# A margin on the operand's due time for steps queued beside a selective scan (one Trainium2 core)

## The chip, the core and the metric

The kernel runs on one core of a Trainium2 chip. The metric is the device time of one execution in microseconds: 9593.26 us is the median of three runs of the kernel before (9591.71 to 9620.02). The profiled execution spans 9618.0 us.

A core has engines with one instruction queue each: PE (matrix multiply), DVE (vector), ACT (scalar functions), POOL (GpSimd) and SP (here it only issues transfers). The order of the instructions in each queue is fixed when the program is built.

## What is computed

The input x has 4 images of 96 channels and 64 x 64 pixels. Four layers follow one another, each added to its input:

```python
x = x + L0(group_norm(x))     # in-projection, 3x3 depthwise conv, selective scan, gate, out-projection
x = x + L1(group_norm(x))     # deformable 3x3 convolution: offsets and mask, bilinear gather, conv
t = t + Fourier(layer_norm(t)); t = t + ffn(layer_norm(t))            # layer 2, on tokens
t = t + linear_attention(layer_norm(t)); t = t + ffn(layer_norm(t))   # layer 3
```

The core of L0 is a recurrence along 4096 positions, for 4 directions k, 192 channels d and 16 states n:

```python
dA = exp(delta * A);  h = dA * h + (delta * u) * B;  y = sum_n(h * C)
```

## The kernel before

**The scan.** `Layer0.scan` (line 776) cuts the recurrence into units of 8 channels x 16 states (128 partitions) by 1024 positions. For each image b, in the order of the directions k = 1, 3, 0, 2, there are 4 steps of 1024 positions by 24 units: 4 x 4 x 4 x 24 = 1536 units. A unit is one instruction or two on each engine: ACT makes the decay `da` by an exponential (866), PE spreads the inflow `db` (872), DVE multiplies it by B (885) and runs the scan (888), POOL saves the last state (895) and multiplies by C (897), and PE adds up over the states (915). Decay and inflow are queued a unit ahead, the product with C two units behind.

**The two streams.** All other work is in two streams of generators made in `layers23`. `ends()` (1617) makes the inputs of the scan for images 0, 1, 2, 3 (`Layer0.before`) and then takes layers 2 and 3 of images 0 to 3 (`Layers23.image`). `middle()` (1627) clears the tables and then for each image takes what follows the scan (`Layer0.behind`) and layer 1 (`Layer1.image`, whose gathers are issued by POOL). A stream gives steps: a few instructions with a cost in us for each engine, `cost(pe, dve, act, pool)`. Most loops are a `pipe` (261) of several chains of such steps, which picks the first chain whose next step may go. A chain may also wait for tokens of buffers (`takes`, `frees`); `Layer0.before` has chains of eight working steps over five chains in flight, with three buffers `ex`, one `lw`, two `rl` and two `du`.

**The clock.** `Clock` (203) holds for each engine the time `ends[engine]` at which what is queued on it will be done, by the written costs. The engines are numbered PE, DVE, ACT, POOL = 0 to 3. After each unit `unit()` moves the due time by PACE = 4.9 and sets `idle`, the end of the scan queued last or the due time, if that is later. Then both streams queue steps until neither has one that may go (`while go()`), and the next unit is queued. When a step may go is told by `has_room` (226): DVE work beside a unit is at most BESIDE = 6.0; the operand (`ready`, the time at which the step before it in its chain is done) must be there when its first engine comes to it, which is the later of `ends[first]` and `idle`; and each engine that it uses may be at most AHEAD (2.0, 1.5, 3.0, 4.0) beyond `now()`. The first engine is looked for in the order PE, ACT, DVE, POOL: a step with PE work has PE as its first engine, a step with ACT and DVE work has ACT.

**Alone.** Before the scan's inputs are there, and after its last unit, `alone()` queues steps by a clock of its own (`clock.own` is a number and not None). After the last unit the streams also get five more PSUM banks. The lists of instructions end up in each queue in the order in which they were made (`in_program_order`).

Lines that the steps below name: 744, 745 and 747 (`w`, `lw`, `rl`), 762 to 768 (`du` in three bf16 parts) in `Layer0.steps`; 1218 and 1227 (gather and its weights) and 1241 and 1249 (transposes and their copy) in `Layer1.sample`; 1417 and 1419 (the last product of the Fourier layer and its addition to t); 1538 (keys and values of the attention, 32 copies for each image).

Of the kernel before, what the change touches and what calls it, by code (L numbers as in the profile page):

```python
# [194 lines left out]

AHEAD = (2.0, 1.5, 3.0, 4.0)

BESIDE = 6.0

PACE = 4.9  # L200
# [2 lines left out]
class Clock:  # L203
# [22 lines left out]
    def has_room(self, work, ready):  # L226
        now = self.now()
        idle = self.idle if self.own is None else self.own
        if self.own is None and work[DVE] and self.beside >= BESIDE:
            return False  # L230
        first = next((e for e in (PE, ACT, DVE, POOL) if work[e]), None)
        if ready > (now if first is None else max(self.ends[first], idle)):
            return False
        return all(not w or e <= now + a for w, e, a in zip(work, self.ends, AHEAD))

# [1450 lines left out]
```

## Time and profile before

| what | value |
|---|---|
| time, median of three runs | 9593.26 us |
| span of the profiled execution | 9618.0 us, 92316 instructions |
| mean granted PE clock | 0.767 |
| scan instructions (line 888) | 1152 of 2347 ns and 384 of 2287 ns, from 356.4 to 8187.7 us |
| product with B (line 885) | 1536 of 1215 ns |
| product with C (line 897) | 1536 of 2389 ns |
| gathers (line 1218) | 1152 of 1228 ns, from 2731.5 to 8839.9 us |

A page of the profile gives the busy time of each engine and then the span in 40 slices, with a digit for the busy tenths of each slice; a slice here is 240 us. The views of the waits say for an engine and line what ended its idle time: "DVE du L768 <- ACT du L766" is DVE standing idle with line 768 at its head until ACT finished line 766. The view of windows gives busy us and instruction counts of each engine in a stretch of time, then the granted PE clock, the share of the transfer engines and GB/s.

### The profile page before, as it was taken

The page shows a single profiled execution, that of the slowest core. Times are in us where ns is not written, and L with a number is a line of the kernel's source. Part 1 is how long each engine was busy: PE and PEld are TensorE (multiplying, and loading weights), DVE is VectorE, ACT ScalarE, POOL GpSimd, SP SyncE. Part 2 cuts the span into 40 slices and gives each one's busy share as a digit, 9 for nine tenths or more (in the row PEclk, how much of TensorE's full clock was granted, in tenths as well). Part 3 has the DMA queues.
Part 4 walks back from the last instruction along what each step waited for, and adds up shares of the span by engine and source line. Part 5 has one row for each costly group of instructions (what it writes and reads, how often), then busy time and mean ns, then how long its engine had stood idle before and what let it go on. Part 6 is the DMA issues. An engine that isn't in the chain of part 4 may idle for free.

```text
span 9618.0 us, 92316 instructions
## 1 busy us (share of the span) xinstructions
PE 6838.2 (71%) x31928; PEld 3124.9 (32%) x31928; DVE 7027.1 (73%) x4707; ACT 4082.4 (42%) x5574; POOL 6730.8 (70%) x4947
## 2 busy tenths in 40 slices
PE   6465855696756667867565787777767787788787
PEld 2111311131212233312122454323335542377474
DVE  0488778877888888778888887788878888332313
ACT  3563656465544333555433233453332345311323
POOL 0696589766889999678899995566989656376101
PEclk8555966696767678967666787877878887989887
DMA  1466676776777778777777787767777776354010
GB/s 48 139 188 168 172 189 193 184 185 177 207 195 191 204 200 206 189 183 205 195 199 203 195 212 172 182 159 190 192 189 198 192 184 168 86 145 130 16 54 11
DMA packets 775819, 1609.47 MB, mean 167 GB/s; under 512 B 247666, under 2 KB 338830, under 8 KB 773239
## 3 DMA queue, kind: packets, MB, share of 16 engines
q10 hardware_dynamic: 300672, 985.79, 40.5%
q1 hardware_dynamic: 400950, 391.20, 14.9%
q0 software_dynamic: 73728, 226.57, 8.8%
q8 instruction: 254, 4.16, 0.2%
q14 instruction: 215, 1.75, 0.1%
HBM read 1346.94 MB, written 256.29 MB: 167 GB/s over the span
## 4 chain that ended last, share of the span: by engine, by line
POOL 29%; PE 25%; DVE 16%; DMA 14%; issue 8%; ACT 5%; ACTq 1%; SPq 1%; DVEq 0%; POOLq 0%
POOL hh L897 13%; POOL g L1218 7%; DVE hh L888 7%; DMA da<-de 4%; DVE db L885 4%; PE pc L657 4%; PE ps L1241 3%; PE f L1332 3%; PE py L915 2%; PE db L872 2%; POOL lw L745 2%; DMA du<-du 2%; PE po L1118 2%; POOL st L895 1%; POOL w L744 1%
## 5 line engine op out<-in xcount | busy, mean ns | idle before, releaser
L897 POOL TENSOR_TENSOR hh<-hh,bc 128x1024 f32<-128x1024 f32 x1536 | 3667.4, 2389 | 341.8 <-DVE hh L888 229.2
L888 DVE TENSOR_TENSOR_SCAN hh<-da,st,db 128x1024 f32<-128x1024 f32 x1152 | 2703.7, 2347 | 365.0 <-ACT da L866 196.7
L872 PE MATMUL db<-du,rep 96*128 96x512 bf16 x3072 | 1172.9, 473 | 1531.8 <-DVE hh L888 1372.3
L866 ACT ACTIVATE da<-da,w_al 128x1024 f32<-128x1024 f32 x1536 | 1734.3, 1145 | 816.8 <-DMA da<-de 457.0
L885 DVE TENSOR_TENSOR db<-db,bc 128x1024 f32<-128x1024 f32 x1536 | 1866.9, 1215 | 278.0 <-PE db L872 275.9
L1218 POOL DMA_INDIRECT g<-table,idx x1152 | 1414.1, 1228 | 308.6 <-issue 226.8
L915 PE MATMUL py<-hh,w_fold 128*32 128x512 f32 x6144 | 1226.2, 809 | 121.6 <-POOL hh L897 98.8
L872 PEld LDWEIGHTS <-rep 96*128 96x128 bf16 x3072 | 275.4, 106 | 2633.9 <-issue 1521.2
L1241 PE MATMUL ps<-w_ident,g 128*96 128x128 f32 x4608 | 729.7, 325 | 342.8 <-DVE g L1227 180.7
L888 DVE TENSOR_TENSOR_SCAN hh<-da,db 128x1024 f32<-128x1024 f32 x384 | 878.1, 2287 | 125.4 <-ACT da L866 73.8
L1227 DVE TENSOR_TENSOR g<-g,wt 128x3456 f32<-128x3456 f32 x128 | 550.6, 4302 | 377.8 <-DMA g<-table,idx 361.4
L1241 PEld LDWEIGHTS ps<-w_ident,g 128*96 128x96 f32 x4608 | 639.6, 153 | 533.6 <-DVE g L1227 231.3
L895 POOL COPY st<-hh 128x1 f32<-128x1 f32 x1152 | 314.6, 273 | 642.6 <-DVE hh L888 619.1
L1249 ACT COPY st<-ps 96x384 f32<-96x384 f32 x384 | 182.1, 476 | 1182.8 <-PE ps L1241 1108.8
L657 PE MATMUL pc<-pad,wc 96*128 96x512 f32 x1152 | 544.0, 620 | 49.2 <-DMA wc<-wc_d 43.7
L1478 POOL CAST xqf<-fl 96x512 fp8e5<-96x512 f32 x64 | 51.2, 806 | 733.3 <-DVE fl L1436 635.5
L744 POOL TENSOR_TENSOR w<-w,ex 128x512 f32<-128x512 f32 x192 | 248.2, 1293 | 383.7 <-ACT w L741 383.2
L915 PEld LDWEIGHTS py<-hh,w_fold 128*32 128x32 f32 x6144 | 173.8, 126 | 719.6 <-issue 372.9
L768 DVE TENSOR_TENSOR du<-ex,du 128x512 bf16<-128x512 f32 x192 | 266.1, 1386 | 190.2 <-ACT du L766 186.6
L734 PE MATMUL pd<-xd,w_dtw 103*64 103x512 f32 (+1 forms) x512 | 316.3, 922 | 68.1 <-DMA w_dtw<-in_dtw 32.0
L747 DVE SCALAR_TENSOR_TENSOR rl<-pd,lw 128x512 f32<-128x512 f32 x192 | 130.0, 677 | 301.3 <-POOL lw L745 296.2
L657 PEld LDWEIGHTS pc<-pad,wc 96*128 96x128 f32 x1152 | 222.8, 198 | 344.6 <-issue 327.4
(241 smaller groups left out, 9366.1 us busy)
## 6 DMA issues: line engine op xcount, KB each, us to landing
da<-de ACTq DMA_DIRECT2D x1536, 512.0 KB
du<-du ACTq DMA_DIRECT2D x384, 192.0 KB
bc<-bcd ACTq DMA_DIRECT2D x128, 512.0 KB
du<-du SPq DMA_DIRECT2D x128, 384.0 KB
y<-yb SPq DMA_DIRECT2D x384, 128.0 KB
de<-rl SPq DMA_DIRECT2D x128, 256.0 KB
m<-in_dft SPq DMA_DIRECT2D x128, 256.0 KB
du<-du SPq DMA_DIRECT2D x128, 192.0 KB
```

Source lines behind the costliest of these rows:

```text
L657: nc.tensor.matmul(pp, lhsT=wc[:, q, g * 128 : (g + 1) * 128], rhs=pad[:, r0 + dy : r0 + dy + NR, dx : dx + W], start=(q == 0), stop=(q == 8),
L744: nc.gpsimd.tensor_sub(w1, w1, ex)
L866: self.net.nc.scalar.activation(u.da, u.da, AF.Exp, scale=self.al[:, a : a + 1])
L872: self.net.nc.tensor.matmul(db[:, h, :], lhsT=self.rep[:96, u.s % 4, :], rhs=u.du[u.s // 4][:, h * CH : (h + 1) * CH], start=True, stop=True,)
L885: nc.vector.tensor_mul(u.db, u.db, u.bc[:, 0, :])
L888: nc.vector.tensor_tensor_scan(u.along(u.hh), u.along(u.da), u.along(u.db), first, ALU.mult, ALU.add)
L895: self.net.nc.gpsimd.tensor_copy(u.state[:, u.n : u.n + 1], u.hh[:, last : last + 1])
L897: self.net.nc.gpsimd.tensor_mul(u.hh, u.hh, u.bc[:, 1, :])
L915: nc.tensor.matmul(py[p0 : p0 + 32], lhsT=self.fold[:, u.i, :], rhs=hc[:, h * CH : (h + 1) * CH], start=u.sums["add"] is None and u.i == 0 ...
L1218: nc.gpsimd.indirect_dma_start(out=g[:, k, :], out_offset=None, in_=self.tables[b % 2], in_offset=bass.IndirectOffsetOnAxis(ap=idx[:, 9 * ...
L1227: nc.vector.tensor_mul(g4, g4, w4.unsqueeze(2).to_broadcast([128, 36, C]))
L1241: nc.tensor.matmul(pt[:, k, :], lhsT=g[:, k0 + k, c * C : (c + 1) * C], rhs=net.ident, is_transpose=True, start=(c == 0), stop=(c == 3),)
```

## The change

A step that is queued beside the scan must now have its operand a margin before the time at which its first engine comes to it. The margin is 0.5 for steps that begin on PE, ACT or POOL and 2.0 for those that begin on DVE. Where a stream runs alone, or where the step is only a wait, it is 0. The purpose is that an operand that comes later on the chip than by the clock doesn't hold up the queue, and the scan's instructions behind it. No instruction is added or removed; only the order in the queues can change.

```diff
 AHEAD = (2.0, 1.5, 3.0, 4.0)
 
+MARGIN = (0.5, 2.0, 0.5, 0.5)
+
 BESIDE = 6.0
@@ Clock.has_room
         first = next((e for e in (PE, ACT, DVE, POOL) if work[e]), None)
-        if ready > (now if first is None else max(self.ends[first], idle)):
+        margin = 0.0 if first is None or self.own is not None else MARGIN[first]
+        if ready + margin > (now if first is None else max(self.ends[first], idle)):
             return False
         return all(not w or e <= now + a for w, e, a in zip(work, self.ends, AHEAD))
```

## The prediction

> **What bounds the kernel now.** I read the page first. Its slices show two stages.
>
> ```profile
> span 9618.0 us, 92316 instructions
> ...
> DVE  0488778877888888778888887788878888332313
> ...
> POOL 0696589766889999678899995566989656376101
> ```
>
> DVE is busy to seven or eight tenths in slices 3 to 34 and then falls to three or less: that is the scan, whose line 888 runs from 356 to 8188 us, 7832 us for 1536 units or 5.10 us a unit. The other 1430 us are the tail, with the streams alone. POOL changes with what stands beside the scan. The view of windows shows this: two stretches of 96 units, then the two halves of the tail (PE, PEld, DVE, ACT, POOL).
>
> ```profile
> 3270.00:3787.00 517.00, 334.76 (x1487) 164.82 (x1486) 440.17 (x256) 171.36 (x222) 475.40 (x350) 0.74 0.78 201
> 7734.00:8188.00 454.00, 353.82 (x1647) 140.70 (x1646) 383.63 (x258) 216.51 (x307) 292.11 (x209) 0.82 0.70 173
> 8188.00:8862.00 674.00, 539.92 (x3618) 405.41 (x3616) 221.94 (x204) 147.44 (x292) 407.69 (x327) 0.88 0.44 121
> 8862.00:9618.00 756.00, 619.27 (x4330) 416.97 (x4328) 224.31 (x316) 237.53 (x469) 84.74 (x67) 0.84 0.11 32
> ```
>
> In the first, with gathers beside it, POOL is 92% busy and a unit takes 517/96 = 5.39 us: POOL is the limit. In the second POOL is 64% busy, DVE 84%, and a unit takes 4.73 us. Three stretches have gathers (2731 to 3847, 4672 to 5744, 6624 to 7533), with POOL at 1025/1116, 994/1072 and 820/909 of the time; they are 3097 of 7832 us, 40%. In the other 60% the DVE's own work, 1.215 + 2.35 = 3.56 us a unit, and its waits set the pace. These are the DVE's longest waits between 800 and 8190 us (total us, times, longest):
>
> ```profile
> DVE db L885 <- PE db L872: 264.6, 130, 28.2
> DVE hh L888 <- ACT da L866: 261.1, 135, 13.2
> DVE du L768 <- ACT du L766: 132.0, 65, 6.9
> DVE g L1227 <- DMA g<-table,idx: 126.6, 41, 7.6
> DVE t L1419 <- PE o L1417: 47.2, 13, 11.8
> DVE hh L888 <- PE py L915: 43.1, 46, 5.4
> DVE rl L747 <- POOL lw L745: 36.6, 25, 3.8
> ```
>
> Lines 885 and 888 wait for the scan's own operands. Lines 768, 1227, 1419 and 747 are steps of the streams that begin on DVE: 342 us in which a step was queued whose operand wasn't there, with the next unit behind it. Before 800 us come 55 us more of line 768 and, the 218.7 us at the start apart, 41 us of line 747. For ACT the same view of the whole span has
>
> ```profile
> ACT du L766 <- POOL ex L764: 220.8, 97, 9.7
> ...
> ACT du L762 <- POOL ex L756: 91.8, 40, 12.8
> ```
>
> steps that begin on ACT and can hold up the decay that is queued behind them.
>
> **The other clock is the stream of the ends.** The copies of the attention's keys (line 1538), 32 for each image, tell where it is (the windows view of that line):
>
> ```profile
> 6400.00:6800.00 400.00, 9.98 (x32) 0.79 0.72 184
> 8000.00:8400.00 400.00, 10.06 (x32) 0.85 0.51 120
> 8800.00:9200.00 400.00, 10.18 (x32) 0.88 0.14 41
> 9200.00:9600.00 400.00, 10.18 (x32) 0.83 0.10 30
> ```
>
> Their first ones are at 6527, 8164, 9037 and 9522. From image 0 to image 1 the stream takes 1637 us beside the scan, from image 2 to 3 485 us alone. When the scan ends the stream has just begun the attention of image 1; it runs on without a gap to the end, while the last gather is done at 8840 and layer 1 of image 3 at 8862, 265 us before image 2 is through layer 3 (9127, line 1509). So the end is set by how far the ends are when the scan ends: what they lose beside the scan comes back in the tail at 485/1637 = 0.30 of its length. The middle stream isn't on that path: its layer 1 ends at 3892, 5777 and 7567 for images 0, 1 and 2 (line 1260), and the next `behind` first computes at 3936, 5924 and 7882 (line 979), when the scan's sums are there.
>
> **What the Trainium skill says.** "TensorE: Matmul & The Clock Gate", section "Architectural detail: the array is 16× 32×32, not 1× 128×128", says that ACT, DVE and GpSimd take their instructions strictly in order. The trace agrees: the 132.0 us of line 768 are idle DVE time although other instructions stand behind. "SBUF — State Buffer", section "SBUF: two separate sides", says that DVE, in an operation with two SBUF inputs, and GpSimd lock each other out of a shared port for a whole instruction. Line 768 has such inputs and takes 665 to 3398 ns (median 1096), which fits; its written cost is 1.2, so operands on the chip can be 2 us behind the clock. That is the size of the DVE margin.
>
> **The change, part by part.** No instruction comes or goes, so the busy times stay. What moves is when a step is queued. `idle` moves once a unit, by 4.9. A step with margin m misses the unit that it would have had in about m/4.9 of the cases and then waits a unit: 2.0/4.9 = 41% of the DVE steps, 0.5/4.9 = 10% of the others; on average its chain is later by m. Inside a unit `ends[first]` can grow and let it go earlier, so this is an upper value.
>
> *Waits saved on DVE.* I take it that a wait gets shorter by up to 2.0 us and that waits are spread like an exponential, so that the share exp(-2.0/mean) stays. Line 768: mean 132.0/65 = 2.03, 37% stays, 83 us saved. Line 747: mean 1.46, 25% stays, 27 saved. Line 1419: mean 3.63, 58% stays, 20 saved. Line 1227: mean 3.09, 52% stays, 60 saved; the clock already gives it 7.0 us after the last gather, so I take half, 30. The 96 us before 800 are partly in the start, when the streams are alone with no margin: 30. Sum 190 us. In the 40% with gathers POOL is the limit and I count 0.3 of it: 190 x (0.60 + 0.40 x 0.3) = 137. From both sides: 60 if chip operands are late by more than the margin, and all of the 342 + 96 = 438, so 315 by the same factor, if every one of these waits goes.
>
> *ACT, PE and POOL with 0.5.* For the ACT waits above (mean 2.3), exp(-0.5/2.3) leaves 80%: some 60 us less ACT idle time, of which I let one in six reach the scan through line 866: 10. On PE nothing is taken: its waits are mostly for the scan itself. On POOL the gathers of one pixel tile follow each other with `ready` equal to `ends[POOL]`. With the margin the next is refused once POOL's end passes `idle` less 0.5, where before it could run on to 4.0 beyond `now`. So POOL is queued less deep; per unit it still takes (4.9 - 2.55)/1.3 = 1.8 gathers by its costs at best. I count nothing for it: fewer gathers a unit make the unit shorter and their number longer, and the middle stream has 44, 147 and 315 us to spare by the times above.
>
> *Steps that go later.* Queued behind a delayed step is nothing, as it isn't in the queue; what waits is its own chain. In `Layer0.steps` a chain has 2 DVE steps and 6 others: 2 x 2.0 + 6 x 0.5 = 7.0 us more latency. Three `ex` buffers share that, 2.3 us a chain; the one `lw` is held over a POOL and a DVE step, 2.5 us. A chain takes 11 us in image 1 (48 chains from 1237 to 1782) and 23 to 25 us in images 2 and 3. But there POOL and DVE are at 88% and 84% (445 and 423 of 503 us from 1330 to 1833), so that latency is mostly hidden by the other chains. A third of 2.4 x 144 chains = 115 us. In layers 2 and 3 an image has about 100 steps that begin on DVE and 370 on PE: 385 us of latency, shared by about three chains in flight, 128 us; for two images beside the scan a third of 256 = 85. Together 200 us of time beside the scan, times 0.30: 60 us more in the tail. From both sides: 0, and (345 + 256) x 0.30 = 180.
>
> *Sum:* -137 - 10 + 60 = -87 us; 9593 - 87 = 9506.
>
> **The rivals.**
>
> 1. *The saved waits outweigh the slower ends*, as worked out: 9506. For it: the stalls stand in the DVE's table, at the engine that sets the pace in 60% of the scan. Chance 0.55.
> 2. *Nearly all of those waits go, and the chains have enough others in flight:* -315, and at -60 from shorter units with fewer gathers, +100 in the tail: about 9320. Against it: 261 and 265 us of waits for ACT and PE stay. Chance 0.10.
> 3. *The wait moves:* the scan gets its DVE slot earlier, but `da` or `db` isn't there; the 569 us on lines 885 and 888 take over most of the 137. With a gain of 60 and a loss of 60: 9593, no change. Chance 0.14.
> 4. *The ends lose more than the scan gains.* The chains are held by their tokens, all of the latency shows: +180, with 80 us gained: 9693, slower. For it: the single `lw`, the single `yt` of the Fourier layer, and three PSUM banks for both streams. Against it: POOL and DVE are near full where these chains run. Chance 0.21.
>
> **How the numbers follow.** Case 1 is the likeliest: 9506. The range goes down to 9380, halfway and more towards case 2, and up to 9660, which takes in case 3 and the milder part of case 4; each end leaves out about one in ten. Faster by over 0.3% (29 us): most of case 1 and case 2, 0.65. Within: 0.14. Slower: 0.21.
>
> **What would show it.** Right: the waits of lines 768, 747 and 1419 between the same points of the scan fall from 216 us to about 85; the last scan instruction comes near 8040 instead of 8188; and the tail after it grows from 1430 to about 1490, with the attention of image 1 later against the scan's end. Wrong: the DVE's idle time stays and shows up at lines 885 and 888 (case 3), or the attention of image 1 begins far past the scan's end and the tail passes 1550 us (case 4), or the gathers of image 2 end after the scan has, so that layer 1 of image 3 and not the ends set the finish.

## The result

The changed kernel takes 9689 us (median of 4 runs, 9675 to 9736) against 9597 us before on the same chip: a ratio of 1.0100, 95% interval 1.0062 to 1.0138. It is slower by about 92 us where 87 us less were forecast, and lies above the range. Single executions of one kernel on one chip scatter by some tens of us (23 of the kernel before on the chip of e1 to e4 took 9583 to 9655 us), and every profile below is of one execution. So a difference of 30 or 40 us in one stretch of two profiles is not clear of scatter.

### Profile after

The page of the changed kernel, the same three lines as before:

```profile
span 9688.9 us, 92274 instructions
...
DVE  0488778887888888778888888898888888232323
...
POOL 0696579866889989678799986576988666275101
```

The engines' busy times are those of before (DVE 7032.9 us for 7027.1, POOL 6731.4 for 6730.8) and so are their numbers of instructions; the 42 fewer in the count are of the kinds that only wait, branch or issue. DVE falls off at the same slice. The last scan instruction ends at 8220 us (8190 before) and 1469 us follow it (1428 before): of 71 us between the two profiled executions 41 lie in the tail and 30 ahead of it, 28 of them in the scan itself. The windows of the changed kernel, chosen as before: a stretch of 96 units with gathers, the last 96 units, and the tail up to and after the end of layer 1 (PE, PEld, DVE, ACT, POOL):

```profile
3279.00:3794.00 515.00, 338.43 (x1457) 157.70 (x1456) 443.23 (x258) 186.95 (x239) 469.59 (x344) 0.75 0.79 203
7771.00:8220.00 449.00, 342.66 (x1871) 144.01 (x1870) 380.71 (x247) 212.97 (x294) 292.06 (x209) 0.84 0.70 173
8220.00:8917.00 697.00, 532.42 (x3245) 391.06 (x3244) 207.52 (x193) 150.10 (x305) 406.24 (x327) 0.86 0.42 117
8917.00:9689.00 772.00, 636.46 (x4785) 433.51 (x4783) 239.75 (x339) 242.40 (x477) 84.84 (x67) 0.89 0.11 32
```

A unit takes no longer than before in the two stretches shown (5.36 and 4.68 us; before 5.39 and 4.73). Of the tail's 41 us, 23 and 16 are in the last two rows. The DVE's waits of the changed kernel between 800 and 8190 us (lines are 3 higher than before, so L891 is 888 and L771 is 768):

```profile
DVE db L888 <- PE db L875: 318.6, 162, 19.9
DVE hh L891 <- ACT da L869: 306.1, 157, 13.4
DVE g L1230 <- DMA g<-table,idx: 107.9, 41, 6.8
DVE hh L891 <- PE py L918: 78.1, 60, 18.3
DVE du L771 <- ACT du L769: 74.0, 37, 8.2
DVE rl L750 <- POOL lw L748: 41.3, 23, 4.2
```

The wait of `du` falls from 132.0 to 74.0 us and that of the Fourier layer's addition (line 1419, 47.2 us before) to 6.1. With line 747 (41.3 for 36.6) the three waits that the prediction watched come to 121 us; they were 216, and 85 had been forecast. But the scan's own three waits rise from 569 to 703 us. These are the windows of the whole scan, before and then changed:

```profile
356.00:8190.00 7834.00, 5473.04 (x23568) 2221.27 (x23568) 6546.17 (x4129) 3542.32 (x4624) 6188.00 (x4507) 0.75 0.73 189
358.00:8220.00 7862.00, 5452.59 (x23477) 2204.07 (x23477) 6548.94 (x4118) 3533.93 (x4599) 6189.05 (x4507) 0.75 0.74 188
```

DVE does the same work in the scan (6546 and 6549 us busy) and is idle for 25 us more, not less.

The copies of the attention's keys, by which the stream of the ends was followed (windows of that line):

```profile
6400.00:6800.00 400.00, 10.21 (x32) 0.77 0.71 182
8000.00:8400.00 400.00, 9.80 (x32) 0.83 0.51 115
8800.00:9200.00 400.00, 10.21 (x32) 0.91 0.19 54
9280.00:9680.00 400.00, 10.22 (x32) 0.91 0.10 30
```

Their first ones are at 6594, 8240, 9135 and 9592. The attention of image 1 began 26 us ahead of the scan's end before; now it begins 20 us after it.

### The profile page after: what moved, and what is told of

Read it like the earlier page. It is cut to its first block, busy times and chain, and to the rows that moved or that the text cites. A ratio compares the mean times of both kernels' runs of the same rounds, so it can differ in the third digit from the quotient of the medians.

```text
span 9688.9 us, 92274 instructions
## 1 busy us (share of the span) xinstructions
PE 6831.1 (71%) x31928; PEld 3111.3 (32%) x31928; DVE 7032.9 (73%) x4707; ACT 4082.9 (42%) x5574; POOL 6731.4 (69%) x4947
## 4 chain that ended last, share of the span: by engine, by line
PE 28%; POOL 20%; DMA 18%; DVE 18%; issue 8%; ACT 5%; ACTq 1%; SPq 1%; DVEq 0%; POOLq 0%
POOL hh L900 9%; DVE hh L891 7%; DMA da<-de 6%; POOL g L1221 5%; DVE db L888 4%; PE pc L660 4%; PE ps L1244 4%; PE f L1335 3%; PE py L918 2%; DMA du<-du 2%; PE db L875 2%; DMA g<-table,idx 2%; PE po L1121 2%; DVE g L1230 1%; POOL lw L748 1%
## 5 line engine op out<-in xcount | busy, mean ns | idle before, releaser
L891 DVE TENSOR_TENSOR_SCAN hh<-da,st,db 128x1024 f32<-128x1024 f32 x1152 | 2703.1, 2346 | 446.5 <-ACT da L869 244.3
L891 DVE TENSOR_TENSOR_SCAN hh<-da,db 128x1024 f32<-128x1024 f32 x384 | 878.2, 2287 | 131.5 <-ACT da L869 76.1
L898 POOL COPY st<-hh 128x1 f32<-128x1 f32 x1152 | 336.8, 292 | 564.4 <-DVE hh L891 535.7
L771 DVE TENSOR_TENSOR du<-ex,du 128x512 bf16<-128x512 f32 x192 | 280.3, 1460 | 146.9 <-ACT du L769 133.3
```

The costliest lines, as they stand in the source:

```text
L891: nc.vector.tensor_tensor_scan(u.along(u.hh), u.along(u.da), u.along(u.db), first, ALU.mult, ALU.add)
L898: self.net.nc.gpsimd.tensor_copy(u.state[:, u.n : u.n + 1], u.hh[:, last : last + 1])
```

## The experiments

Three theories went into them. ENDS: the time follows how far the stream of the ends is when the scan ends; a margin on its own steps delays it, and a margin on the middle stream lets it through. MOVED WAIT: the waits that the margin saves on DVE come back at lines 885 and 888. LUCK: any new order scatters by some 90 us. Where an expectation speaks of the ordering clock, it means the time at which the kernel's own `Clock` has the last step done when the program is built: 9331 for before, 9388 for the changed kernel.

The table has all runs. "Scan's end" and "tail" are of one profiled execution each, "keys" is the start of the attention of image 1 less the scan's end, and "clock" is the ordering clock's end less that of before. Where a ratio is turned into us below, it is taken of the median of before on the same chip; the plain difference of the two medians can be up to 20 us away from it. The kernel before itself had medians from 9600 to 9648 on the chips of these runs, so scan ends are best compared between runs of one chip: e1 to e4, e5 to e8, e9 to e11, e12 to e14.

| run | what | ratio to before, 95% | scan's end | tail | keys | clock |
|---|---|---|---|---|---|---|
| before | | 1 | 8190 | 1428 | -26 | 0 |
| after | margins 0.5, 2.0, 0.5, 0.5 | 1.0100 (1.0062 to 1.0138) | 8220 | 1469 | +20 | +57 |
| e1 | DVE 2.0 alone | 1.0157 (1.0129 to 1.0186) | 8203 | 1587 | +201 | +160 |
| e2 | without DVE's | 1.0041 (1.0028 to 1.0055) | 8264 | 1395 | -201 | -52 |
| e3 | middle stream only | 0.9846 (0.9817 to 0.9875) | 8222 | 1235 | -598 | -240 |
| e4 | ends only | 1.0214 (1.0183 to 1.0245) | 8180 | 1639 | +380 | +224 |
| e5 | without PE's | 0.9980 (0.9968 to 0.9993) | 8158 | 1484 | -91 | -3 |
| e6 | middle only, POOL's alone | 0.9927 (0.9899 to 0.9956) | 8263 | 1320 | -436 | -160 |
| e7 | before, short loads of `da` | 0.9745 (0.9713 to 0.9776) | 7958 | 1444 | -29 | 0 |
| e8 | after, short loads of `da` | 0.9790 (0.9763 to 0.9817) | 7916 | 1508 | +20 | +57 |
| e9 | ends asked first, no margin | 0.9905 (0.9888 to 0.9921) | 8266 | 1209 | -919 | -240 |
| e10 | ends first, all margins | 1.0054 (1.0037 to 1.0071) | 8324 | 1319 | -618 | -157 |
| e11 | middle only, PACE 5.0 | 0.9930 (0.9913 to 0.9947) | 8349 | 1178 | -947 | -136 |
| e12 | ends only, DVE's alone | 1.0126 (1.0096 to 1.0157) | 8235 | 1541 | +90 | +107 |
| e13 | ends only, without DVE's | 1.0057 (1.0036 to 1.0079) | 8142 | 1556 | +181 | +141 |
| e14 | middle only, DVE 3.0 | 0.9854 (0.9821 to 0.9887) | 8271 | 1229 | -688 | -268 |

### Which stream: e3 and e4

```diff
# e3; e4 has 0 in place of 1, the number of the stream in net.streams
+        net.clock.which = net.streams.index(self)        # Stream.step
-        margin = 0.0 if first is None or self.own is not None else MARGIN[first]
+        margin = 0.0 if first is None or self.own is not None or self.which != 1 else MARGIN[first]
```

> All four margins as in the change, but only for steps of the middle stream (behind, layer 1); steps of the ends have none. ENDS: the ends get the room that the middle stream leaves; by the ordering clock 240 us earlier than before, so about 9360, with the attention of image 1 well inside the scan and the tail under 1250, set by the gathers of image 3. MOVED WAIT: a third of the effect of the change, as the du and rl steps of the ends keep their waits: 9600 to 9630. LUCK: 9500 to 9700.

> All four margins as in the change, but only for steps of the ends; steps of the middle stream have none. ENDS: the ends lose twice, by their own later steps and because the middle stream takes the room: by the ordering clock 224 us later than before, so about 9800, with a tail over 1600. MOVED WAIT: most of the DVE waits that the margin can save are of the ends (lines 768, 747, 1419), so the loss is that of the whole change: about 9680, the tail unchanged. LUCK: 9500 to 9700.

Measured: 0.9846, that is about 148 us less (136 by the medians), and 1.0214, about 205 us more (222 by the medians). Both go the way of ENDS, and both lie outside LUCK's 9500 to 9700 (9468 and 9826). The same margins in the same code gain on one stream and lose on the other. The windows of the keys' line for images 1, 2 and 3 show where. First with the margin on the middle stream:

```profile
7400.00:7800.00 400.00, 9.96 (x32) 0.79 0.69 172
8600.00:9000.00 400.00, 10.19 (x32) 0.80 0.36 101
9200.00:9600.00 400.00, 10.18 (x32) 0.87 0.03 11
```

and with the margin on the ends:

```profile
8400.00:8800.00 400.00, 10.22 (x32) 0.83 0.44 125
9000.00:9400.00 400.00, 10.22 (x32) 0.88 0.10 30
9400.00:9800.00 400.00, 10.22 (x32) 0.87 0.10 30
```

The attention of image 1 (first row) begins at 7624 in one and at 8560 in the other, 598 us ahead of the scan's end and 380 us after it. The scan ends within 42 us of the same place (8222 and 8180); the tails are 1235 and 1639 us. With the margin on the middle stream the tail is close to the least that this order can have: layer 1 of image 3 ends at 8926, and what layers 2 and 3 then still need for image 3 took 491 us in the kernel before, together 9417 of the 9457 us of this execution. e3 gave 136 to 148 us of the clock's 240.

### Which margin: e1, e2, e5, e12, e13

```diff
-MARGIN = (0.5, 2.0, 0.5, 0.5)
+MARGIN = (0.0, 2.0, 0.0, 0.0)      # e1; e2: (0.5, 0.0, 0.5, 0.5); e5: (0.0, 2.0, 0.5, 0.5)
# e12: (0.0, 2.0, 0.0, 0.0) and e13: (0.5, 0.0, 0.5, 0.5), both for the ends only, as in e4
```

> Margins (0, 2.0, 0, 0): the DVE margin alone. Theory ENDS (the time follows how far the stream of the ends is when the scan ends; a margin on that stream's steps delays it): this is the costly part of the change, the clock that orders the queues puts the end 160 us later than before, so about 9750, with the attention of image 1 wholly in the tail and the tail near 1600. Rival MOVED WAIT (the waits saved on DVE come back at lines 885 and 888 and lengthen the scan, which is all of the loss): the scan takes about 7860 as after, the tail stays near 1430 to 1470, about 9640 to 9690. Rival LUCK (any new order scatters by some 90 us): anything from 9500 to 9700.

> Margins (0.5, 0, 0.5, 0.5): the change without its DVE margin. ENDS: the small margins thin out the gathers of the middle stream, which begin on POOL with no time in hand, and leave room for the ends; by the ordering clock 52 us earlier than before, so about 9540 on the chip, with the tail shorter than 1430. MOVED WAIT: without the DVE margin no DVE wait is saved and none moves, so waits on lines 768, 747 and 1419 as before (273 us in the scan) and a time like before, 9590. LUCK: 9500 to 9700.

> Margins (0, 2.0, 0.5, 0.5): the change without its PE margin. By the ordering clock its end is where that of before is (3 us earlier), while DVE, ACT and POOL keep their margins. ENDS (the progress of the ends at the scan's end sets the time): about as before, 9570 to 9640, with the attention of image 1 starting inside the scan. MOVED WAIT (the DVE margin's saved waits come back in the scan and are the loss): as the change, about 9690. LUCK: anything from 9500 to 9700.

DVE's margin alone costs 1.57%, as ENDS had it (9773 us against about 9750 expected). It also does on DVE what it is for. These are the DVE's waits of e1 in the scan (from 356 to 8190 us):

```profile
DVE hh L891 <- ACT da L869: 397.2, 186, 16.1
DVE db L888 <- PE db L875: 257.7, 145, 19.3
DVE du L771 <- ACT du L769: 105.4, 56, 10.2
DVE g L1230 <- DMA g<-table,idx: 89.1, 35, 8.5
DVE rl L750 <- POOL lw L748: 60.0, 37, 5.2
DVE hh L891 <- PE py L918: 53.8, 50, 6.3
```

And these are those of before in the same span of time:

```profile
DVE hh L888 <- ACT da L866: 270.5, 142, 13.2
DVE db L885 <- PE db L872: 265.6, 131, 28.2
DVE du L768 <- ACT du L766: 165.2, 82, 6.9
DVE g L1227 <- DMA g<-table,idx: 126.6, 41, 7.6
DVE rl L747 <- POOL lw L745: 60.6, 37, 5.0
DVE t L1419 <- PE o L1417: 47.2, 13, 11.8
DVE hh L888 <- PE py L915: 43.1, 46, 5.4
```

The four waits of side steps were 400 us before; here the first three of them are 255 and the Fourier addition is under 7. But the scan's own waits go from 579 (270.5 + 265.6 + 43.1) to 709 us, nearly all of it at line 888 behind `da` (270.5 to 397.2). What the margin saved, some 140 us, was waited out again: MOVED WAIT is right for the waits within the scan, whose end is 13 us later than before and not some 140 us earlier. Most of the cost of e1 is in the tail, 1587 us.

e2 missed. Its tail is shorter than before (1395), as ENDS said, but its scan is 74 us longer and the sum 0.41% slower, not faster. Its DVE waits on gathers are longer:

```profile
DVE g L1230 <- DMA g<-table,idx: 181.0, 51, 9.5
```

against 126.6 before. But the 74 us are not waits alone. Over the scan of e2 the view of windows has

```profile
356.00:8264.00 7908.00, 5455.46 (x23679) 2231.11 (x23678) 6590.35 (x4138) 3555.56 (x4655) 6189.70 (x4508) 0.75 0.73 187
```

so DVE is busy for 44 us more than before (6590 for 6546) and idle for 30 more. With the ends further on (the attention of image 1 starts 201 us ahead of the scan's end), more DVE time falls beside the scan. In e3, whose ends are further on still, it is busy for 6608 us there, and in e13, whose ends lag, for 6526. The ordering clock can't tell this: it takes the scan at 4.9 us a unit whatever lies beside it.

e5 came out like before (0.998), in the range that ENDS gave. But it didn't get there by the way that ENDS says. Its tail of 1484 us is no shorter than the changed kernel's 1469, although the attention of image 1 begins 91 us ahead of the scan's end. What is shorter is its scan, 7800 us for 7862. There DVE waits less for PE:

```profile
DVE db L888 <- PE db L875: 258.9, 136, 17.5
DVE hh L891 <- PE py L918: 32.8, 36, 2.3
```

292 us, where the changed kernel has 397 (318.6 and 78.1). So without PE's margin the loss is gone, and by these two profiles, taken on different chips, it is the scan that is shorter and not the tail. Why PE's margin, together with the others, makes the scan's operands from PE later was not tested. That the time of e5 agrees with ENDS looks like luck.

> The DVE margin of 2.0 alone, and only on the ends. The prediction's term for later steps was 0 to 180 us in the tail with 60 taken, and within it DVE steps counted 2 x 2.0 of 7.0 us of a chain. ENDS: by the ordering clock 107 us later than before, so a ratio near 1.010, the tail 1520 to 1550. If the small margins of the other engines are what delays the ends, this stays at 0.998 to 1.003.

> The margins of 0.5 on PE, ACT and POOL alone, and only on the ends. ENDS: by the ordering clock 141 us later than before: many small delays on some 370 PE steps an image weigh more than the DVE's large ones, a ratio near 1.014, the tail 1550 to 1580. If the DVE's margin is the costly one, this stays at 1.000 to 1.005.

On the ends alone both parts of the margin lengthen the tail: 1541 us with DVE's and 1556 with the small ones. They differ in the scan. The wait of line 888 for `da`, first with DVE's and then with the small ones:

```profile
DVE hh L893 <- ACT da L871: 377.9, 177, 12.0
DVE hh L893 <- ACT da L871: 278.0, 139, 10.3
```

The second is like before; the scans end at 8235 and 8142. So the run with DVE's is slower (1.0126 against 1.0057), though its tail is not longer. Both expectations had the tails about right and the order of the two wrong.

### Where the saved waits went: e7 and e8

```diff
-        u.da = sp.tile([128, T], F32, name=f"da{u.key}", tag="da", bufs=5)
+        # five tiles, each loaded in full (n = T) the first time, n = 16 after that
+        u.da = self.das[self.fetched % 5]
-        nc.scalar.dma_start(u.da, src.unsqueeze(0).to_broadcast([NS, D8, T]))
+        nc.scalar.dma_start(u.da[:, :n], src[:, :n].unsqueeze(0).to_broadcast([NS, D8, n]))
```

> Before, with its order unchanged, but each unit's load of delta into da brings 16 of its 1024 positions; the rest is what an earlier unit left there (five tiles that are loaded in full once). That leaves out most of the recurrence's delta. MOVED WAIT, in the form that the scan waits for the landing of da, so that time saved on DVE is waited out at line 888: the waits of line 888 on ACT da fall from 270 us to under 100, and the scan gets shorter by 150 us or more, to 7680 or less. If the scan is held elsewhere (POOL, or DVE's side work), it stays within 50 us of 7834.

> The changed kernel with the same shortened loads of da (order unchanged, most of delta left out). If da's landing is what took the DVE margin's savings back, then without it the scan of the changed order is shorter than that of the order before by the 100 us of side waits saved: e8 minus e7 in the scan is -60 to -120 us, against +28 with the full loads. If the savings are taken back by something else (PE's db, ACT's queue, POOL), the difference stays between 0 and +40.

Both kernels leave out most of delta, so that they time the recurrence without computing it; their order is kept. With short loads the scan in the order of before takes 7602 us (356 to 7958), 232 less than with full ones, although that is a comparison across chips. On one chip, the scan in the changed order is 43 us shorter than in the order before (7559 from 357 to 7916, against 7602); with full loads it was 28 us longer. The waits of lines 885 and 888 and of the gathered pixels in the scan, first in the order before and then in the changed order (total us, times, longest):

```profile
DVE db L892 <- PE db L879: 192.6, 112, 20.8
DVE hh L895 <- ACT da L873: 130.4, 151, 4.5
DVE g L1234 <- DMA g<-table,idx: 38.5, 20, 7.1
```

```profile
DVE db L895 <- PE db L882: 218.5, 142, 8.5
DVE hh L898 <- ACT da L876: 161.7, 148, 6.0
DVE g L1237 <- DMA g<-table,idx: 38.4, 17, 4.2
```

The waits of line 888 for `da` still rise, by 31 us, and line 885's by 26. The two differences, 28 longer and 43 shorter, are 71 us apart, which speaks for the landing of `da` taking back a part of what DVE's margin saves. It is not shown firmly: each difference is of two single executions, the 43 us are short of the 60 to 120 expected, and short loads also cut the waits for the gathers (126.6 us before, 38.5 here). What takes the rest was not tested further. The whole time of e8 is still above that of e7, 9437 against 9402 us, and there it is the tail alone that is longer (1508 against 1444).

### Order of asking, and the way to a faster version: e6, e9, e10, e11, e14

```diff
# e6: e3 with MARGIN = (0.0, 0.0, 0.0, 0.5); e14: e3 with (0.5, 3.0, 0.5, 0.5); e11: e3 with PACE = 5.0
# e9, on before; e10, on after:
-            return any([stream.step() for stream in reversed(streams)])
+            return any([stream.step() for stream in (streams if clock.own is None else reversed(streams))])
```

> Only POOL's margin of 0.5, and only on the middle stream, where it meets the gathers, each of which follows the one before with no time in hand. ENDS: this one margin is enough to let the ends through; by the ordering clock 160 us earlier than before; the run with all margins on the middle stream got 136 of its 240 us, so about 9510, with a tail near 1300. If instead the PE and DVE margins on the middle stream did the work there, this stays at 9590 to 9610.

> Before, with no margin at all, but beside the scan the stream of the ends is asked for a step ahead of the middle stream (before asks the middle one first). ENDS: it is the competition of the two streams for engine time, POOL's above all, and for the three banks that matters, not the margin; by the ordering clock 240 us earlier than before, the same as the margin on the middle stream alone, which measured a ratio of 0.985: so 0.98 to 0.99, with side waits on DVE as before. If the margin on the middle stream gained by late operands no longer blocking queues, then the order of asking alone gives at most half of that: 0.993 to 1.0.

> The changed kernel (all margins, both streams) with the ends asked first. ENDS: the same margins still delay the ends; by the ordering clock 83 us later than ends first with no margin, so a ratio 0.007 to 0.01 above that run's. MOVED WAIT: the margins cost what their moved waits cost in the scan, some 30 us, with the tail unchanged: 0.003 above.

> The margins on the middle stream alone, and PACE 5.0 in place of 4.9, so that the clock gives the streams 2% more time beside each unit. The chip's unit takes 5.1 us anyway. If the scan on the chip does not get longer for it, the ends are further at its end and the tail is set by the gathers of image 3 alone: ratio 0.975 to 0.985. If the scan is filled by what is queued beside it, it lengthens by some 100 us and gives back the gain: 0.985 to 0.995.

> Margins (0.5, 3.0, 0.5, 0.5) on the middle stream alone. By the ordering clock 27 us earlier than with 2.0 for DVE. If more margin on the multiplication of the gathered pixels keeps saving DVE waits on line 1227 (127 us before, 148 with 2.0), then 0.980 to 0.984; if the tail is by now set by the gathers of image 3 and the attention after it, no gain over 0.9846: 0.983 to 0.988.

e9 has no margin at all and gains 0.95%, just outside the 0.98 to 0.99 that ENDS gave, its attention of image 1 starting 919 us ahead of the scan's end: the competition of the two streams is enough for a gain of this kind. Its scan ends at 8266, though, and its ratio is above that of e3 with a tail of about the same length. e6 shows that POOL's margin alone on the middle stream gives half of e3's gain. DVE's waits for the gathers' landing in the scan, in e6 and then in e3:

```profile
DVE g L1232 <- DMA g<-table,idx: 195.8, 56, 8.7
DVE g L1232 <- DMA g<-table,idx: 144.4, 51, 9.3
```

They are shorter with all four margins on that stream, and shorter again with 3.0 for DVE (102.8 in e14). The multiplication of the gathered pixels is a step of the middle stream, so DVE's margin is the likely cause; e6 and e3 also differ in PE's and ACT's, so it is not shown. And in e14 the scan's own three waits are 640 us where e3, on another chip, has 539: once more what is saved on a side step is waited at lines 885 and 888. e10 lies 0.0149 above e9, more than ENDS had for the margins (0.007 to 0.01): 110 us in the tail and 58 in the scan. e11 went the second way of its expectation, with the scan the longest of all (8349). e14 is not apart from e3. The fastest kernel that computes everything is e3: the margins of the change, on the middle stream alone, 9468 us.

## Why the prediction was wrong

**Where the miss lies.** The forecast had the scan 147 us shorter and the tail 60 longer. By the two profiled executions the scan got 28 us longer and the tail 41. Nearly all of the miss is in the scan; that the tail's 41 is near 60 is luck, as the parts below show.

**What bounds the kernel.** Right in the main: the end is set by the ends stream, and the tail goes with its place at the scan's end. e4 and e3 move that place by 406 us later and 572 earlier and the tail by 211 longer and 193 shorter, 0.52 and 0.34 us for each, where 0.30 had been taken from the attention's spacing. Behind the scan the ends still share the engines with layer 1 of image 3; that a late us costs more there than in the stretch where they are alone would fit, but was not tested. The start of the attention of image 1 is a rough mark of that place: e5 has it 65 us earlier than before and a tail 56 us longer.

**Waits saved on DVE: 137 us.** This step failed. The waits on DVE steps did fall, between 800 and 8190 us by 113 (342 to 229), against 160 reckoned there ahead of the factor for the gathers. Taking them as time of the scan was wrong: the scan's own waits rose by 134 (569 to 703), and the scan did not get shorter. That is the mechanism of rival 3, which had been given 0.14. The profile before hinted at it: lines 885 and 888 already waited 569 us for the scan's own operands, more than the 342 of the side steps. An earlier slot on DVE doesn't make the queues that deliver these operands faster.

**ACT waits: 10 us.** The smaller term of the same kind rested on 60 us less ACT idle time, and ACT's two waits did fall, from 311 us in the scan (219.2 and 91.8) to 254 (206.9 and 46.7). It went the way of the DVE waits: no shorter scan came of it.

**Small margins on the middle stream.** "I count nothing for it", said of POOL, was the second failure. The prediction was right that the middle stream is not on the path to the end, but it takes room beside the scan that the ends could use, and POOL's margin on it alone is worth about 70 us (e6). The prediction expected fewer gathers a unit. The traces don't show that: the 288 gathers of image 0 stretch over some 215 units before and in e6, and those of image 1 over 206 and 174. By which way the margin lets the ends through stays open.

**Steps that go later: 60 us, from 0 to 180.** Mis-sized, by two errors that nearly cancel: the cost to the ends was taken too small, and the room that a held-back middle stream gives them was left out. With the margins only on the ends the tail grew by 211 us (e4), above the upper end. The place at the scan's end moved by 406 us, twice the 200 reckoned, and the exchange rate was 0.52 and not 0.30. How much of the 406 is the chains' own latency and how much is room that the middle stream took is not separated. In the change as made, the margins on the middle stream give most of that back (tails of 1639 us in e4, 1469 in the changed kernel) and 41 us are left.

**Which margin.** The working held DVE's 2.0 to be the larger part of the latency in `Layer0.steps` (4.0 of 7.0 us) and about half of it in layers 2 and 3 (200 of 385). That both count for the tail is right: 1541 and 1556 us (e12, e13).

**The rivals.** Rival 4 (9693, chance 0.21) has the number, 9689, by luck: its marks were the attention of image 1 far past the scan's end and a tail over 1550 us, and they are 20 us and 1469; the loss in the tail is 41 and not 180, and its 80 us of gain do not exist. What happened is rival 3's moved wait in the scan and a part of rival 4's delay in the tail. LUCK does not explain the large steps: the clock's end and the measured ratio fall on the same side in 10 of the 12 rows with full loads and a clock over 3 us from before's, all but e2 and e10, whose scans are longer than the clock can know. But the change's own 92 us are a small sum, and scans of different orders end anywhere from 8142 to 8349 us, partly by the work beside them and partly for reasons that were not found. So that the change moved waits instead of saving them is shown; that it lost 92 us rather than 30 or 120 is not explained.

## What to carry to other kernels

A wait removed on the busiest engine was worth only what the next wait in the same loop left: look first at how long the loop's own operands are already late. When two side streams share a planner's room, find out which of them ends last; here, a rule that holds steps back was good for the other one and bad for that one. A planner that takes its main loop at a fixed pace ranks orders by the side streams alone, so a gain of its clock counts only as far as the loop's real pace doesn't change.

## What was not expected of the hardware

Cutting the one broadcast load of each unit (512 KB) to 16 of 1024 positions took 232 us off a scan of 7834 (across chips), while DVE's waits for `da` fell by only 140 (270.5 to 130.4). Other waits fell with it: DVE's for the gathers by 88 (126.6 to 38.5) and those of line 885 for PE by 73 (265.6 to 192.6). DVE's busy time in the scan stayed (6556 us for 6546), and the share of the transfer engines fell from 0.73 to 0.34. So the large loads cost other work too, and not only the instruction that reads them; by what way was not tested. And DVE's waits on the gathers were longer where POOL's margin stood without DVE's: 126.6 us before, 181.0 in e2 and 195.8 in e6.
